# A graph layer, a mixer and an expert layer in one kernel: the targets' own rows as three bf16 parts, records zeroed ahead

## The chip, the cores and the metric

The kernel runs on one core of a Trainium2 chip. The metric is the device time of one execution in microseconds (us), the median of several executions. The engines are named as in the profile: PE is TensorE's matmuls and PEld its weight loads, DVE is VectorE, ACT is ScalarE, POOL is GpSimd, SP is SyncE, which here only issues DMAs.

## The reference

3125 nodes have 512 features each, and 50000 edges join them. The layer normalizes the rows, adds a message-passing layer and a linear-attention mixer, and then a layer of eight experts of which each row takes two. The change touches the message passing alone:

```python
edge_dst, edge_src = (edge_index[0], edge_index[1])
p0, p1 = split_irreps(irrep_linear(x, W_pre0, b_pre0, W_pre1))
pd0 = p0[edge_dst]
ip1 = einsum('eum,eum->eu', p1[edge_dst], p1[edge_src]) / 3.0
s0 = concatenate([pd0, pd0, ip1], -1)
w = ssp(edge_attr @ W_f1) @ W_f2 * (ssp(s0 @ W_s1) @ W_s2)
...                                                      # out0, out1 from w, x[edge_src] and edge_sh
out = segment_sum(edge_feat, edge_dst, num_segments=N)
```

For every edge one needs the row of its target (`pd0` through `W_s1` is 32 numbers, `p1` is 384) and the row of its other end. All is float32.

## The kernel before

The work has three parts in time.

**The sort (up to about 565 us).** The 3125 targets are cut into 25 tiles of 125, each tile into two halves of up to 64 targets. The kernel counts on the chip which half each edge belongs to and gives it a place, by matmuls of bf16 one-hots on PE and comparisons on DVE. Then each edge's record (48 floats: 4 spherical numbers, the index of the other end, the index of the target, its place in the half tile, and 32 hidden numbers from the edge's attributes) is written to its place in the DRAM table `recs` by indirect DMAs that POOL issues, 128 edges each (`place`, L529). All these puts wait for two DMAs that zero part of `recs` (`cleared`, L183): only the last quad of each tile and the quads for overflow. In the same stretch PE, DVE and ACT compute the node tables: `rows_d` (416 floats a node: the 32 and the 384 from above) and `rows_s` (896 floats), the mixer and the sums so far. The last DMAs of `place` follow without PE.

**The edges (about 565 to 1697 us).** Edges are worked on in *pairs* of two columns of 128 edges, one column from each half of a tile; two pairs make a *quad*, 104 in all. Eight pairs (four quads) belong to each of the 25 tiles, and eight pairs more, with a tile looked up at run time, hold what overflows (`late_tiles`). The order of the instructions on PE, ACT, DVE and POOL is that of the program (`manual_schedule`): one step `s` of a loop issues a stage of several different pairs, so that a pair passes through the stages over some 14 steps. SP's order is the scheduler's. The stages, with the names that matter:

- `load` brings the quad's records to `Q.rec`; `targets` brings a tile's 125 own rows from `rows_d` to `own` (SP, two DMAs of 64 rows, three buffers).
- `clear` (DVE, L1109) masks records of places that no edge took, with `real_slot`: what was not zeroed in DRAM is whatever lay there.
- `which` (DVE, L1142) makes the one-hot `one` of each edge's place among the 64 targets; `over` (PE L1150, ACT L1152) turns the first pair's into `oneT`.
- `fetch` gathers `gx` (rows of the other end, for both pairs) and `gd` (target rows, for the second pair alone) by indirect DMAs on POOL.
- `own_rows` (PE, L1163) spreads the tile's own rows over the first pair's edges by matmul with `oneT`, so that these need no gather; two row groups of 64 run side by side.
- `products` (DVE), `turn` (PE, L1182), `hidden` (PE, L1196 to L1211; L1206 is the targets' 32 numbers, for the first pair again from `own` with `oneT`), `softplus` (ACT).
- `scaled` (ACT, L1250) makes `ones`, the one-hot times each spherical number; `weigh` (PE L1262, L1263; ACT L1265; DVE L1266) the weights; `feats` (DVE L1280, L1284) the features; `gather_up` (PE, L1304) sums them by target into PSUM.

Matmuls whose operands are float32 are two PE instructions in the trace, those in transposing form and those in bf16 one.

**The experts (about 1697 us to the end)**, which the change leaves alone.

Of the kernel before, what the change touches and what calls it, by code (L numbers as in the profile page):

```python
# [17 lines left out]
P = 128  # L18
# [8 lines left out]
G = 4  # L27
# [24 lines left out]
def gnn_mix_moe_kernel(ctx: ExitStack, tc: tile.TileContext, a: dict, out: bass.AP):  # L52
# [41 lines left out]
    nc.vector.tensor_scalar(ident, jp, 0.0, None, op0=ALU.is_equal)  # L94
    after = const.tile([P, P], F32, name="after")
    nc.vector.tensor_scalar(after, jp, 0.0, None, op0=ALU.is_gt)
    ones = const.tile([P, P], F32, name="ones")
    nc.vector.memset(ones, 1.0)
    eps = const.tile([P, 1], F32, name="eps")
# [5 lines left out]
    real_slot = const.tile([P, NFIX + NOV_MOST, PR], I32, name="real_slot")  # L105


    rows_d = dram.tile([N + 2, HID + 3 * MUL], F32, name="rows_d")
# [34 lines left out]
    with ExitStack() as c1:  # L143
# [27 lines left out]
        for r in range(4):  # L171
# [5 lines left out]

        zero = tmp.tile([P, 3 * P], F32, name="zero")
        nc.vector.memset(zero, 0.0)
        by_quad = recs.rearrange("(q p i) f -> p q (i f)", p=P, i=G)  # L180
        per = PER // PR
        cleared = [
            nc.gpsimd.dma_start(by_quad[:, qs, :], zero[:, : G * REC].unsqueeze(1).to_broadcast([P, n, G * REC]))  # L183
            for qs, n in (
                (slice(per - 1, NFIX // PR, per), NG), (slice(NFIX // PR, (NFIX + NOV_MOST) // PR), NOV_MOST // PR),
            )
        ]
        for part in (slice(0, HID), slice(HID, HID + 3 * MUL)):
            nc.gpsimd.dma_start(rows_d[N:, part], zero[:2, : part.stop - part.start])
# [572 lines left out]
        w1t = c4.enter_context(tc.tile_pool(name="w1t", bufs=1, reuse_waits="tile"))  # L762


        def fixed_real():

            is_real = w1t.tile([P, NG, PER, 2], F32, name="is_real")
            nc.vector.tensor_tensor(
                is_real, slot_no[:, :PER].unsqueeze(1).unsqueeze(3).to_broadcast([P, NG, PER, 2]),
                held.unsqueeze(2).to_broadcast([P, NG, PER, 2]), op=ALU.is_lt,  # L770
            )
            nc.vector.tensor_single_scalar(
                real_slot[:, :NFIX, :].rearrange("p s k -> p (s k)"),
                is_real.rearrange("p b j k -> p (b j k)"), -1.0, op=ALU.mult,
            )
# [20 lines left out]
        def over_tiles(k):  # L796

            begun = w1t.tile([P, NOV], F32, name="begun", bufs=2)
            nc.vector.tensor_scalar(begun, pair_no, own_of[:, 2 + k : 3 + k], None, op0=ALU.is_ge)
            nc.vector.tensor_scalar(steps, ones, own_of[:, k : k + 1], None, op0=ALU.mult)  # L800
            ps = psum.tile([P, NOV], F32, name="ps_ov", tag="mm")
            nc.tensor.matmul(ps, steps[:NG, :], begun[:NG, :], start=True, stop=True)
            nc.vector.tensor_tensor(is_over, slot_no, ps, op=ALU.is_lt)
            late = w1t.tile([P, NOV], I32, name="late")
            nc.vector.tensor_single_scalar(late, is_over, -1.0, op=ALU.mult)
            nc.vector.tensor_copy(real_slot[:, NFIX:, k], late[:, :NOV_MOST])
# [88 lines left out]
        def lengths(c):  # L895
# [11 lines left out]
            8: [(composed,)], 9: [(fixed_real,), (over_steps,)], 10: [(over_tiles, 0)], 11: [(over_tiles, 1)],  # L907
        }
        for c in range(NCH):
            pieces.setdefault(2 * c, []).append((lengths, c))  # L910
# [167 lines left out]
    with ExitStack() as c2:  # L1078
# [53 lines left out]
        def targets(bs):  # L1132

            own = gat.tile([P, HID + 3 * MUL], F32, name="own", bufs=3)
            for k, b in enumerate(bs):
                nc.sync.dma_start(own[k * HT : (k + 1) * HT, :], rows_d[bass.ds(b * TG + k * (HT - 1), HT), :])
            return own

        def which(Q):

            Q.one = work.tile([P, G, HT], F32, name="one", bufs=5)
            nc.vector.tensor_tensor(  # L1142
                Q.one, lane[:, :HT].unsqueeze(1).to_broadcast([P, G, HT]),
                Q.rec[:, :, 6:7].to_broadcast([P, G, HT]), op=ALU.is_equal,
            )

        def over(Q):

            ps = ps_a.tile([P, G, P], F32, name="ps_one", tag="turned")
            nc.tensor.transpose(ps[:, 0, :], Q.one[:, :PR, :].rearrange("p k t -> p (k t)"), ident)  # L1150
            Q.oneT = work.tile([P, P], F32, name="oneT", bufs=4)
            nc.scalar.copy(Q.oneT, ps[:, 0, :])  # L1152

        def own_rows(R):

            if R.j == 1:
                R.gd = R.Q.gd[:, :, HID:]
                return
            ps = ps_a.tile([P, PR, D], F32, name="ps_gd")
            R.gd = ps[:, :, : 3 * MUL]  # L1160
            for k in range(PR):
                h = slice(k * HT, (k + 1) * HT)
                nc.tensor.matmul(  # L1163
                    R.gd[:, k, :], R.Q.oneT[h, :], R.own[h, HID:], start=True, stop=True,
                    tile_position=(k * HT, 0),
                )

        def products(R):

# [22 lines left out]
        def hidden(Q):  # L1192

            Q.ps = ps_a.tile([P, G, P], F32, name="ps_h", tag="turned")
            for i in range(G):
                nc.tensor.matmul(  # L1196
                    Q.ps[i * HID : (i + 1) * HID, 0, :], Q.rec[:, i, 8:USED], ident,
                    start=True, stop=True, tile_position=(0, i * HID),
                )
            for i in range(G):  # L1200
                h = slice(i % PR * HT, (i % PR + 1) * HT)
                if i < PR:
                    of, to, at = Q.gd[:, i, :HID], ident, 0
                else:
                    of, to, at = Q.pairs[0].own[h, :HID], Q.oneT[h, :], i % PR * HT
                nc.tensor.matmul(  # L1206
                    Q.ps[i * HID : (i + 1) * HID, 1, :], of, to, start=True, stop=False,
                    tile_position=(at, i * HID),
                )
            for i in range(G):  # L1210
                nc.tensor.matmul(  # L1211
                    Q.ps[i * HID : (i + 1) * HID, 1, :], w_s1c, Q.ip[:, i, :], start=False, stop=True,
                    tile_position=(0, i * HID),
                )
# [94 lines left out]
        def tile_of(engine, at):  # L1309

            return engine.value_load(at, min_val=0, max_val=NG - 1)
# [14 lines left out]
        with tc.manual_schedule(engines=steady):  # L1326
# [7 lines left out]
            def pair(at):  # L1334

                return [pairs[at]] if 0 <= at < n_pairs else []

            def late_tiles(at):

                return [pair_tile[0:1, k, at - NFIX : at - NFIX + 1] for k in range(2)]  # L1340
# [11 lines left out]
            for s in range(-LEAD - 5, n_pairs + 1):  # L1352
# [6 lines left out]
                for R in pair(s + LEAD + 3):  # L1359
                    at = s + LEAD + 3  # L1360
                    if at >= NFIX and R.j == 1:
                        continue
                    if at >= NFIX:
                        R.own = targets([tile_of(nc.sync, v) for v in late_tiles(at)])
                    elif at % PER == 0:
                        R.own = targets([at // PER] * 2)
                    else:
                        R.own = pairs[at - 1].own
                kept(s - 1)
                for Q in due(s + 2):  # L1370
                    softplus2(Q)
                for R in pair(s + 7):
                    products(R)
                for Q in due(s + LEAD + 1):
                    q = quads.index(Q)
                    clear(Q, real_slot[:, PR * q : PR * (q + 1), :])
                    which(Q)
                for Q in due(s + LEAD):
                    over(Q)
# [33 lines left out]
        with tc.If(some > NOV_MOST):  # L1413
            with tc.For_i(NOV_MOST // PR, (some + 1) // PR, 1) as i:
# [10 lines left out]
                for j in range(PR):  # L1425
                    R = Pair(Q, j)
                    fetch(Q, j)
                    if j == 0:
                        R.own = targets([tile_of(nc.sync, whose[:, k, j : j + 1]) for k in range(2)])
                    own_rows(R)  # L1430
                    products(R)
                turn(Q)
# [506 lines left out]
```

## Time and profile before

| | |
|---|---|
| median of 3 runs | 2573.27 us (2565.25 to 2579.46) |
| profiled execution | 2575.68 us, its span 2573.9 us |
| busy share of the span: PE, DVE, ACT, POOL | 91%, 64%, 49%, 59% |
| first put of a record, last put | 46.24 us, 564.21 us |
| PE's last matmul of the sort, its first of the edges | 479.89 us, 569.49 us |
| stretch 605 to 1650 us: PE, DVE, ACT, POOL busy | 1045, 970, 791, 668 us |
| `gather_up`, PE L1304 | 3328 matmul instructions, 493.8 us |
| `own_rows`, PE L1163, 900 to 1500 us | 228 matmul instructions of 535 ns, 52.2 us |

The span is that of the instructions; the execution's own time is 1.8 us more. Matmuls are pipelined, so their times overlap and the sum of a group's durations is more than the time from its first start to the next group's; starts are what to read.

### The profile page before, as it was taken

What the parts mean: (1) busy time and instruction counts of PE and PEld (TensorE: products, weight loads), DVE (VectorE), ACT (ScalarE), POOL (GpSimd) and SP (SyncE); (2) the same over time, 40 slices, a digit from 0 to 9 for tenths busy, and PEclk for the clock granted to TensorE, in tenths of its full rate; (3) what the DMA queues carried; (4) which work ended last, traced back from release to release, by engine and by line L of the source; (5) the groups of instructions that cost most, each with busy time, mean ns of one, the idle gap of its engine ahead of it and who ended that gap; (6) DMA issues with size and microseconds to landing.
All of it is one profiled execution on the core that took longest, in us unless ns stands there. A gap on an engine that the chain in (4) does not pass through costs nothing. (4 is left out here: it accounts for less than half of the span.)

```text
span 2573.9 us, 46654 instructions
## 1 busy us (share of the span) xinstructions
PE 2347.7 (91%) x16977; PEld 1522.1 (59%) x16977; DVE 1634.8 (64%) x3130; ACT 1254.0 (49%) x3444; POOL 1529.1 (59%) x1488
## 2 busy tenths in 40 slices
PE   6888999408999999999999999984999999999998
PEld 4654456304444444444444444463888888888887
DVE  8887444207999999999999999976222222222222
ACT  2665512105777777777777777752222222222221
POOL 3777767776666666666666666413555555555552
PEclk7999999758999999999999999997999999999999
DMA  4665889528777777777777777545315325857454
GB/s 145 189 209 198 303 294 312 191 65 262 231 229 232 229 230 228 231 229 231 230 228 227 233 228 231 175 164 209 107 51 183 131 56 192 332 186 258 140 171 143
DMA packets 188092, 521.94 MB, mean 203 GB/s; under 512 B 55421, under 2 KB 84166, under 8 KB 177104
## 3 DMA queue, kind: packets, MB, share of 16 engines
q0 software_dynamic: 110224, 397.55, 48.2%
q1 hardware_dynamic: 71296, 115.05, 13.6%
q10 hardware_dynamic: 6336, 6.28, 0.8%
q8 instruction: 137, 2.24, 0.3%
q14 instruction: 99, 0.81, 0.1%
HBM read 586.07 MB, written 104.25 MB: 268 GB/s over the span
## 5 line engine op out<-in xcount | busy, mean ns | idle before, releaser
L1127 POOL DMA_INDIRECT gx<-rows_s,rec x416 | 445.5, 1071 | 326.5 <-DVE ft L1284 217.7
L1304 PE MATMUL ps_s<-ft,ones 128*64 128x256 f32 (+1 forms) x3328 | 493.8, 439 | 10.0 <-DVE acc L1318 9.9
L1250 ACT ACTIVATE ones<-one,rec 128x64 f32<-128x64 f32 x1664 | 429.5, 337 | 0.0
L1800 PE MATMUL ps_f<-h,we 128*128 128x128 f32 x3328 | 394.4, 277 | 1.2 <-DVE h L1815 1.2
L1813 ACT ACTIVATE h<-ps_f,bias 128x128 f32<-128x128 f32 x312 | 114.5, 368 | 575.2 <-PE ps_f L1800 558.7
L529 POOL DMA_INDIRECT recs<-again,at_i x335 | 326.3, 974 | 113.9 <-issue 78.9
L1800 PEld LDWEIGHTS ps_f<-h,we 128*128 128x128 f32 x3328 | 379.8, 192 | 3.1 <-DVE h L1815 1.6
L1284 DVE TENSOR_TENSOR ft<-wt,gx 128x768 f32<-128x768 f32 x416 | 378.3, 951 | 0.0
L1815 DVE TENSOR_SCALAR h<-ps_f,bias 128x128 f32<-128x128 f32 x312 | 108.6, 350 | 422.7 <-PE ps_f L1800 419.0
L1304 PEld LDWEIGHTS ps_s<-ft,ones 128*64 128x64 f32 x3328 | 222.2, 136 | 228.3 <-issue 148.5
L1720 POOL DMA_INDIRECT we<-w_rows,w_at x208 | 211.6, 1017 | 215.4 <-PE ps_y L1832 93.3
L1266 DVE TENSOR_TENSOR wt<-wt,wb 128x1024 f32<-128x1024 f32 x208 | 253.2, 1217 | 59.7 <-ACT wt L1265 59.2
L1123 POOL DMA_INDIRECT gd<-rows_d,rec x208 | 252.6, 1214 | 64.6 <-issue 64.3
L1265 ACT COPY wt<-wa 128x1024 f32<-128x1024 f32 x208 | 211.3, 1016 | 126.2 <-PE wb L1263 126.2
L1262 PE MATMUL wa<-w_f,hT 32*128 32x512 f32 x832 | 236.8, 640 | 0.0
L1263 PE MATMUL wb<-w_s,hT 32*128 32x512 f32 x832 | 235.8, 640 | 0.0
L1800 PEld LDWEIGHTS ps_f<-xt,we 128*128 128x128 f32 x1664 | 195.4, 193 | 25.5 <-issue 23.7
L1800 PE MATMUL ps_f<-xt,we 128*128 128x128 f32 x1664 | 195.8, 276 | 0.7 <-ACT xt L1748 0.7
L1832 PE MATMUL ps_y<-we,h 128*128 128x512 f32 x416 | 192.4, 605 | 0.1
L1182 PEld LDWEIGHTS ps_ip<-ident,prod 128*128 128x128 f32 x1248 | 136.6, 142 | 78.7 <-ACT oneT L1152 77.2
L1182 PE MATMUL ps_ip<-ident,prod 128*128 128x128 f32 x1248 | 161.6, 280 | 0.7 <-ACT oneT L1152 0.7
L1280 DVE TENSOR_TENSOR ft<-wt,gx 128x512 f32<-128x512 f32 x208 | 144.0, 692 | 7.1
(394 smaller groups left out, 3282.2 us busy)
## 6 DMA issues: line engine op xcount, KB each, us to landing
w_rows<-in_Wh SPq DMA_DIRECT2D x24, 1024.0 KB
rows_s<-r SPq DMA_DIRECT2D x24, 448.0 KB
rec<-recs SPq DMA_DIRECT2D x104, 96.0 KB
w_rows<-in_Wo SPq DMA_DIRECT2D x8, 1024.0 KB
lined<-rec SPq DMA_DIRECT2D x12, 672.0 KB
again<-lined POOLq DMA_DIRECT2D x12, 672.0 KB
gx<-rows_s,rec POOLq DMA_INDIRECT x416
xs<-acc POOLq DMA_DIRECT2D x25, 256.0 KB
```

The source lines that it names most:

```text
L529: put = nc.gpsimd.indirect_dma_start(out=recs[:, :], out_offset=bass.IndirectOffsetOnAxis(ap=at_i[:m, t : t + 1], axis=0), in_=again[c][:m ...
L1123: nc.gpsimd.indirect_dma_start(out=Q.gd[:, i - 2, :], out_offset=None, in_=rows_d[:, :], in_offset=bass.IndirectOffsetOnAxis(ap=reci[:, i, ...
L1127: nc.gpsimd.indirect_dma_start(out=Q.gx[:, i, :], out_offset=None, in_=rows_s[:, :], in_offset=bass.IndirectOffsetOnAxis(ap=reci[:, i, 4:5 ...
L1182: nc.tensor.matmul(ps[:, i, :], Q.prod[:, i, b * P : (b + 1) * P], ident, is_transpose=True, start=(b == 0), stop=(b == 2),)
L1250: nc.scalar.activation(R.ones[:, k, c, :], R.Q.one[:, i, :], AF.Copy, scale=R.Q.rec[:, i, c : c + 1])
L1262: nc.tensor.matmul(wa[:, k, :], Q.hT[r, 0, :], w_f2[r, :], start=True, stop=True)
L1263: nc.tensor.matmul(wb[:, k, :], Q.hT[q, 1, :], w_s2[q, :], start=True, stop=True)
L1266: nc.vector.tensor_mul(R.wt, R.wt, wb)
L1284: nc.vector.tensor_mul(R.ft[:, k, MUL : 7 * MUL].rearrange("p (b c u) -> p b c u", b=2, c=3), w[:, k, :, 1, :].unsqueeze(2).to_broadcast([ ...
L1304: nc.tensor.matmul(to, R.ones[:, k, m, :], what, start=(first and m == 0), stop=(last and m == 3), tile_position=(0, k * HT),)
L1720: nc.gpsimd.indirect_dma_start(out=dst, out_offset=None, in_=src, in_offset=bass.IndirectOffsetOnAxis(ap=at[:, j : j + 1], axis=0), bounds ...
L1800: nc.tensor.matmul(pss[f], ws[l][:, k, f * P : (f + 1) * P], h[:, k, :], start=(k == 0), stop=(k == 3))
```

## The change

Four things are done.

1. The own rows of a tile are split into three bf16 parts that sum to them: ACT copies the rows to bf16 (`own_high`), DVE subtracts that from the rows (`own_rest`), ACT copies what is left to bf16 (`own_middle`), DVE subtracts again into the third part (`own_low`). This is done once for each tile, in four steps of the loop, ahead of use. The float32 rows have two buffers, the parts three.
2. The one-hot `one` and its turned form `oneT` are bf16. `over` is a bf16 matmul with a bf16 identity instead of a float32 transpose. `own_rows` and the targets' part of `hidden` accumulate three bf16 matmuls in place of each float32 one.
3. All 104 quads of `recs` are zeroed at the start, by four DMAs.
4. `clear`, `real_slot` and `fixed_real` go from the loop: the records are used as they come.

```diff
+    ident_b = const.tile([P, P], BF16, name="ident_b")
+    nc.vector.tensor_copy(ident_b, ident)
...
-        by_quad = recs.rearrange("(q p i) f -> p q (i f)", p=P, i=G)
-        per = PER // PR
+        n_zero = (NFIX + NOV_MOST) // PR * G * REC
+        step_z = zero.shape[1]
+        by_part = recs[: n_zero * P // REC, :].rearrange("(p i) f -> p (i f)", p=P)
         cleared = [
-            nc.gpsimd.dma_start(by_quad[:, qs, :], zero[:, : G * REC].unsqueeze(1).to_broadcast([P, n, G * REC]))
-            for qs, n in (
-                (slice(per - 1, NFIX // PR, per), NG), (slice(NFIX // PR, (NFIX + NOV_MOST) // PR), NOV_MOST // PR),
-            )
+            nc.gpsimd.dma_start(
+                by_part[:, i * n_zero // 4 : (i + 1) * n_zero // 4].rearrange("p (a b) -> p a b", b=step_z),
+                zero.unsqueeze(1).to_broadcast([P, n_zero // 4 // step_z, step_z]),
+            )
+            for i in range(4)
         ]
...
+        class Own:
+            def __init__(self, bs):
+                self.rows = gat.tile([P, OWN], F32, name="own", bufs=2)
+                for k, b in enumerate(bs):
+                    nc.sync.dma_start(
+                        self.rows[k * HT : (k + 1) * HT, :], rows_d[bass.ds(b * TG + k * (HT - 1), HT), :]
+                    )
+        def own_high(O):
+            O.parts = gat.tile([P, 3, OWN], BF16, name="own_b", bufs=3)
+            nc.scalar.copy(O.parts[:, 0, :], O.rows)
+        def own_rest(O):
+            nc.vector.tensor_sub(O.rows, O.rows, O.parts[:, 0, :])
+        def own_middle(O):
+            nc.scalar.copy(O.parts[:, 1, :], O.rows)
+        def own_low(O):
+            nc.vector.tensor_sub(O.parts[:, 2, :], O.rows, O.parts[:, 1, :])
...
-            Q.one = work.tile([P, G, HT], F32, name="one", bufs=5)
+            Q.one = work.tile([P, G, HT], BF16, name="one", bufs=5)
...
-            nc.tensor.transpose(ps[:, 0, :], Q.one[:, :PR, :].rearrange("p k t -> p (k t)"), ident)
-            Q.oneT = work.tile([P, P], F32, name="oneT", bufs=4)
+            nc.tensor.matmul(
+                ps[:, 0, :], Q.one[:, :PR, :].rearrange("p k t -> p (k t)"), ident_b, start=True, stop=True
+            )
+            Q.oneT = work.tile([P, P], BF16, name="oneT", bufs=4)
...
-            for k in range(PR):
-                h = slice(k * HT, (k + 1) * HT)
-                nc.tensor.matmul(
-                    R.gd[:, k, :], R.Q.oneT[h, :], R.own[h, HID:], start=True, stop=True,
-                    tile_position=(k * HT, 0),
-                )
+            for part in range(3):
+                for k in range(PR):
+                    h = slice(k * HT, (k + 1) * HT)
+                    nc.tensor.matmul(
+                        R.gd[:, k, :], R.Q.oneT[h, :], R.own.parts[h, part, HID:], start=(part == 0),
+                        stop=(part == 2), tile_position=(k * HT, 0),
+                    )
...
-                    of, to, at = Q.pairs[0].own[h, :HID], Q.oneT[h, :], i % PR * HT
+                    terms = [Q.pairs[0].own.parts[h, part, :HID] for part in range(3)]
+                    to, at = Q.oneT[h, :], i % PR * HT
...
+                for R in split(s + LEAD + 1):
+                    own_rest(R.own)
+                for R in split(s + LEAD):
+                    own_low(R.own)
...
-                    q = quads.index(Q)
-                    clear(Q, real_slot[:, PR * q : PR * (q + 1), :])
                     which(Q)
...
                 for R in pair(s + 2):
                     scaled(R, 1)
+                for R in split(s + LEAD + 2):
+                    own_high(R.own)
+                for R in split(s + LEAD + 1):
+                    own_middle(R.own)
```

More of the change, by code (lines that the diff above doesn't have):

```diff
@@ L104, in gnn_mix_moe_kernel @@
     pair_tile = const.tile([P, 2, NOV_MOST], I32, name="pair_tile")
-    real_slot = const.tile([P, NFIX + NOV_MOST, PR], I32, name="real_slot")
     rows_d = dram.tile([N + 2, HID + 3 * MUL], F32, name="rows_d")
@@ L179, in gnn_mix_moe_kernel @@
         nc.vector.memset(zero, 0.0)
-        by_quad = recs.rearrange("(q p i) f -> p q (i f)", p=P, i=G)
-        per = PER // PR
+        n_zero = (NFIX + NOV_MOST) // PR * G * REC
+        step_z = zero.shape[1]
+        assert n_zero % (4 * step_z) == 0
+        by_part = recs[: n_zero * P // REC, :].rearrange("(p i) f -> p (i f)", p=P)
         cleared = [
-            nc.gpsimd.dma_start(by_quad[:, qs, :], zero[:, : G * REC].unsqueeze(1).to_broadcast([P, n, G * REC]))
-            for qs, n in (
-                (slice(per - 1, NFIX // PR, per), NG), (slice(NFIX // PR, (NFIX + NOV_MOST) // PR), NOV_MOST // PR),
+            nc.gpsimd.dma_start(
+                by_part[:, i * n_zero // 4 : (i + 1) * n_zero // 4].rearrange("p (a b) -> p a b", b=step_z),
+                zero.unsqueeze(1).to_broadcast([P, n_zero // 4 // step_z, step_z]),
             )
+            for i in range(4)
         ]
@@ L762, in gnn_mix_moe_kernel @@
         w1t = c4.enter_context(tc.tile_pool(name="w1t", bufs=1, reuse_waits="tile"))
[L765 to L770, printed above, removed]
-            )
-            nc.vector.tensor_single_scalar(
-                real_slot[:, :NFIX, :].rearrange("p s k -> p (s k)"),
-                is_real.rearrange("p b j k -> p (b j k)"), -1.0, op=ALU.mult,
-            )
         is_over = w1t.tile([P, NOV], F32, name="is_over")
@@ L805, in over_tiles @@
             nc.vector.tensor_single_scalar(late, is_over, -1.0, op=ALU.mult)
-            nc.vector.tensor_copy(real_slot[:, NFIX:, k], late[:, :NOV_MOST])
             nc.sync.dma_start(late_real[k], late)
@@ L906, in gnn_mix_moe_kernel @@
             6: [(through, w_nn[0][:, 1, :], w_nn[0][:, 0, :], w_o[0])], 7: [(through, w_nn[1][:, 1, :], w_nn[1][:, 0, :], w_o[1])],
-            8: [(composed,)], 9: [(fixed_real,), (over_steps,)], 10: [(over_tiles, 0)], 11: [(over_tiles, 1)],
+            8: [(composed,)], 9: [(over_steps,)], 10: [(over_tiles, 0)], 11: [(over_tiles, 1)],
         }
@@ L1130, in fetch @@
                 )
[L1132 to L1137, printed above, removed]
+        OWN = HID + 3 * MUL
+        class Own:
[14 more added lines that the diff above has]
+            nc.vector.tensor_sub(O.parts[:, 2, :], O.rows, O.parts[:, 1, :])
         def which(Q):
-            Q.one = work.tile([P, G, HT], F32, name="one", bufs=5)
+            Q.one = work.tile([P, G, HT], BF16, name="one", bufs=5)
             nc.vector.tensor_tensor(
@@ L1160, in own_rows @@
             R.gd = ps[:, :, : 3 * MUL]
-            for k in range(PR):
-                h = slice(k * HT, (k + 1) * HT)
-                nc.tensor.matmul(
-                    R.gd[:, k, :], R.Q.oneT[h, :], R.own[h, HID:], start=True, stop=True,
-                    tile_position=(k * HT, 0),
-                )
+            for part in range(3):
[5 more added lines that the diff above has]
+                    )
         def products(R):
@@ L1202, in hidden @@
                 if i < PR:
-                    of, to, at = Q.gd[:, i, :HID], ident, 0
+                    terms, to, at = [Q.gd[:, i, :HID]], ident, 0
                 else:
-                    of, to, at = Q.pairs[0].own[h, :HID], Q.oneT[h, :], i % PR * HT
[L1206 to L1209, printed above, removed]
+                    terms = [Q.pairs[0].own.parts[h, part, :HID] for part in range(3)]
+                    to, at = Q.oneT[h, :], i % PR * HT
+                for j, of in enumerate(terms):
+                    nc.tensor.matmul(
+                        Q.ps[i * HID : (i + 1) * HID, 1, :], of, to, start=(j == 0), stop=False,
+                        tile_position=(at, i * HID),
+                    )
             for i in range(G):
@@ L1336, in pair, with split @@
                 return [pairs[at]] if 0 <= at < n_pairs else []
+            def split(at):
+                return [R for R in pair(at) if (at % PER == 0 if at < NFIX else R.j == 0)]
             def late_tiles(at):
@@ L1363, in gnn_mix_moe_kernel @@
                     if at >= NFIX:
-                        R.own = targets([tile_of(nc.sync, v) for v in late_tiles(at)])
+                        R.own = Own([tile_of(nc.sync, v) for v in late_tiles(at)])
                     elif at % PER == 0:
-                        R.own = targets([at // PER] * 2)
+                        R.own = Own([at // PER] * 2)
                     else:
@@ L1428, in gnn_mix_moe_kernel @@
                     if j == 0:
-                        R.own = targets([tile_of(nc.sync, whose[:, k, j : j + 1]) for k in range(2)])
+                        R.own = Own([tile_of(nc.sync, whose[:, k, j : j + 1]) for k in range(2)])
+                        own_high(R.own)
+                        own_rest(R.own)
+                        own_middle(R.own)
+                        own_low(R.own)
                     own_rows(R)
```

## The prediction

> **What bounds the kernel now.** I read the page's slices first, then the windows by stage, the timelines of PE and DVE in the middle of the edge stage, and POOL's timeline up to that stage. Slices of the page:
> ```profile
> PE   6888999408999999999999999984999999999998
> DVE  8887444207999999999999999976222222222222
> PEclk7999999758999999999999999997999999999999
> ```
> Window of the edge stage (columns: stretch, its length, then busy time and instructions of PE, PEld, DVE, ACT and POOL, the granted clock, DMA share, GB/s):
> ```profile
> 605.00:1650.00 1045.00, 1045.00 (x8794) 508.36 (x8794) 970.45 (x1287) 791.33 (x2399) 667.93 (x594) 1.00 0.75 230
> ```
> PE is busy all of 1045 us, at full clock; DVE 93%, ACT 76%, POOL 64%. A busy PE may still be one that waits between its matmuls, so the timeline of PE, and one line of its weight loads:
> ```profile
> 1006.53 0.41 PE L1206 MATMUL ps_h<-oneT,own 64*32 64x128 f32 x4
> 1006.87 0.43 PE L1211 MATMUL ps_h<-ip,w_s1c 128*32 128x128 f32 x8
> ...
> 1009.53 0.92 PE L1163 MATMUL ps_gd<-own,oneT 64*128 64x384 f32 x4
> 1010.38 0.33 PE L1150 MATMUL ps_one<-ident,one 128*128 128x128 f32 x1
> 1010.64 0.69 PE L1262 MATMUL wa<-w_f,hT 32*128 32x512 f32 x1
> ```
> ```profile
> 1009.53 0.30 PEld L1163 LDWEIGHTS ps_gd<-own,oneT 64*128 64x128 f32 x4 [0.38 <-issue]
> ```
> Each group starts where the one before it ends. The same group returns after 10.57 us (L1262 at 1000.07 and 1010.64), which is one quad of edges (four half tiles, two pairs): over 0.26, weigh 1.07, turn 1.46, gather_up 2.30, weigh 1.07, hidden 1.26, gather_up 2.30, own_rows 0.85. PE is the bound of this stage, and what is saved on PE shortens it until DVE binds. DVE over the same quad:
> ```profile
> 1002.31 1.22 DVE L1266 TENSOR_TENSOR wt<-wt,wb 128x1024 f32<-128x1024 f32 x1 [0.59 <-ACT wt L1265]
> ...
> 1006.98 0.32 DVE L1109 TENSOR_TENSOR rec<-rec,real_slot 128x160 int32<-128x160 int32 x1
> 1007.40 0.42 DVE L1142 TENSOR_TENSOR one<-lane,rec 128x256 f32<-128x256 f32 x1
> ...
> 1008.99 0.69 DVE L1280 TENSOR_TENSOR ft<-wt,gx 128x512 f32<-128x512 f32 x1
> 1009.60 1.82 DVE L1284 TENSOR_TENSOR ft<-wt,gx 128x768 f32<-128x768 f32 x2
> ```
> Its one wait in a quad is 0.59 us, so it has 9.98 us of work: only 0.59 us behind PE.
>
> The second stretch that matters is before it. POOL places the edges' records, one put each 1.26 us:
> ```profile
> 46.24 1.04 POOL L529 DMA_INDIRECT recs<-rec,at_i  x1 [37.97 <-DVE at_i L375]
> 337.09 0.96 POOL L529 DMA_INDIRECT recs<-again,at_i  x1 [6.83 <-PE ps_nn L1002]
> 569.68 1.05 POOL L1127 DMA_INDIRECT gx<-rows_s,rec  x1 [4.56 <-DVE one L1142]
> ```
> The last put is at 564, 84 us after PE's last matmul of that stage. Between 328 and 360 the puts wait 12.4 us for PE (2.30, 6.83, 2.19 and 1.08), so a later first put is absorbed up to 12 us, but a later PE chain is not.
>
> **PE, part by part.** The rates come from the sort, where both kinds stand side by side:
> ```profile
> 63.50 0.31 PE L339 MATMUL ps_at<-xT,after_b 128*128 128x350 bf16 x1
> 63.65 0.29 PE L340 MATMUL ps_at<-seen,ones_b 128*128 128x300 bf16 x1
> 63.78 0.31 PE L343 MATMUL ps_at<-starts,part_of 128*128 128x350 bf16 x1
> ...
> 64.35 1.88 PE L642 MATMUL ps_kx<-xn,kf 128*128 128x512 f32 x4
> 66.07 1.05 PE L419 MATMUL ps_h<-w_f,ea 128*128 128x128 f32 x8
> ```
> Bf16: 0.15 us for 350 columns and 0.13 for 300, 0.43 ns a column. F32: 1.72 us for four instructions of 512, 0.84 ns a column, and two instructions to a matmul. From bf16 to f32 and back costs nothing there.
> - own_rows: two f32 passes of 384 columns (its two row groups run side by side) are 0.645 us of the 0.85, so 0.20 is the group's own start and end. Three bf16 passes are 0.49, with the 0.20 again 0.69: 0.16 less.
> - hidden's own part: 0.34 us, of which 2 x 128 columns f32 0.215, so 0.125 fixed. Three bf16 passes 0.165, in all 0.29: 0.05 less.
> - over: 0.26, of which one pass of 128 f32 columns 0.107. In bf16 0.055: 0.05 less.
>
> In sum 0.26 us a quad. Bounds: if a bf16 load of 128 columns takes none of the fixed part, own_rows and over give another 0.05 each, 0.36; if the fixed part is paid for every pass, there is a loss (rival). I take 0.26, since the four f32 loads of L1163 above take 0.30 us in all and so lie beside matmuls that run 0.85: the later passes' loads are hidden, and each bf16 pass (0.16 us) is as long as half of that. 1045 / 10.57 = 99 quads: **-26 us**.
> [...]
>
> **DVE and ACT.** The clear of L1109 goes, 104 times: 0.42 us from its start to the next. Added for each target tile (25 fixed, 4 late; a tile lasts four quads) are two subtractions of 128x416 on DVE and two copies on ACT. No row mixes bf16 with f32 in a subtraction; by L1280 (0.61 us from start to start for 512) it is 0.50, and I bound it at 0.4 and, twice that row, 1.0. So DVE does 9.98 - 0.42 + 2 x 0.50 / 4 = 9.81 us a quad (10.06 at the dear end), under PE's new 10.31. The one-hot in bf16 has f32 operands still: same 0.42. ACT's copies, by L1190's 0.56 for 512, are 0.46: 0.23 a quad on an engine with 2.6 us idle. They stand behind `scaled` at the end of a step; queued behind them is ACT's copy of wa, then DVE's wt; feats ends at 1005.99 and its gather starts at 1007.23, and that 1.24 us covers half a microsecond. Without that cover it would be 0.5 us for 25 tiles, 12 us. The four late tiles' splits fall into the last steps of full PE: 1.0 us more on DVE in each of four quads (9.56 + 1.0 = 10.56 against 10.31), **+1**. The tail after 1650 is DVE's own and keeps its length. SP's loads of own rows have two buffers instead of three, but these are free after own_low, not after four quads: nothing waits longer.
> At the start, the gathers no longer wait for clear and one (568.56 to about 569.6, the 4.56 us row): **-1**.
>
> **The zeros.** Four DMAs on POOL's queue write all 104 quads, 128 x 13 x 384 x 4 bytes each, 10.2 MB instead of 2.85. POOL issues them in some 4 us of the 38 it sits idle. The DMA engines while they wrote the old zeros:
> ```profile
> 4.00:14.00 10.00, 4.35 (x13) 1.88 (x13) 9.37 (x26) 0.00 (x0) 2.88 (x5) 1.00 1.03 330
> ```
> Full, at 330 GB/s, of which the zeros some 270. From 14 to 22 us the share was 0.59, from 22 to 46 0.30. At 270 GB/s the new zeros end at 4 + 38 = 42 us, before the first put (which waits for them). But all that is loaded meanwhile for the sort goes at a fraction: `ea` for PE at 21.80, x for DVE at 36.73, W_kT for PE at 40.07, all ahead of the first put on their in-order engines. The bounds are 0 and, if nothing of ea lands before 42, +20. I take **+4**, near the lower end, since ea, sh and W_kT also moved while the DMA was full.
> [...]
>
> Sum: -26 + 1 - 1 + 4 = -22. The profiled execution took 2575.7 (span 2573.9), 2.4 above the median, so 2553.7 there and **2551** as a median.
>
> **Rivals.**
> 1. Slower: every accumulating pass shows its load. Where: own_rows and hidden, two further passes each. If a pass adds half the group's fixed share, own_rows is 0.49 + 0.20 + 2 x 0.10 = 0.89 and hidden's part 0.41: with over -0.05, +0.06 a quad, +6 us, with the zeros about 2583. If all of it, 1.09 and 0.54: +0.39 a quad, +39, about 2616. It eats the saving from 0.065 us a pass. Against it: the loads of L1163. Chance 0.10.
> 2. DVE binds: its 0.59 us wait for ACT stays, as it hangs on weigh and the copy of wa, which keep their length. Then a quad is 9.56 + 0.25 + 0.59 = 10.40: 17 us saved instead of 26, 2560. Against: PE reaches weigh earlier after a shorter own_rows and over. Chance 0.13.
> 3. The zeros starve the sort: +20 instead of +4, 2567. For: x and ea are needed before 42 us. Chance 0.10.
> That the change does not do what it says is excluded by the order of the built instructions: no clear is left, each own_rows is six loads and six matmuls.
>
> **How the numbers follow.** The forecast has 0.67, its own range 2536 (PE at 0.36 a quad, zeros free) to 2562. Measurable from no change is about 0.5%, 13 us: faster is below 2560, slower above 2586. Faster: 0.63 of the forecast and 0.07 of rival 2, 0.70. Slower: 0.09, the most of rival 1 and a little for zeros far slower than any row. Same: the rest, 0.21. The range is 2534 to 2574: up to rival 3, leaving out rival 1.
>
> **What would show it.** Right: own_rows from start to next group 0.69, over 0.21, hidden's part 0.29, a quad of 10.31 with PE still full and DVE at 95%; first put at about 50 us, last at about 568. Wrong: weight loads of L1163 that start only when the matmul before has ended; idle PE ahead of gather_up; a first put well behind 50.

## The result, and the profile after

The changed kernel takes 2538.72 us (median of 4 runs, 2536.73 to 2541.63) against 2570.20 for the kernel before, run beside it (4 runs): 31.5 us less, a ratio of 0.9875, 95% interval 0.9855 to 0.9894. The forecast was 2551, its range 2534 to 2574. The profiled execution took 2537.24 us, its span is 2535.5: 38.4 less than before's 2573.9, where the sum of the prediction had 22 less. The profiled pair differs by more than the medians, since before's profiled execution lay 5.5 us above its median and after's 1.5 below.

The slices of the changed kernel's page look like those of before:

```profile
PE   5888989507999999999999999966999999999998
...
PEclk7999999857999999999999999987999999999999
```

The window of the edge stage (stretch, length, busy time and instructions of PE, PEld, DVE, ACT, POOL, granted clock, DMA share, GB/s):

```profile
605.00:1600.00 995.00, 995.00 (x9089) 493.00 (x9090) 955.58 (x1227) 805.02 (x2428) 654.94 (x588) 1.00 0.77 239
```

PE is still full and DVE at 96%: PE still sets the pace. From the first gather of the edges to the end of the last sum kept, before took 1132.6 us (569.68 to 1702.29) and after 1092.1 (569.93 to 1662.05). So 40.5 us came off this stage; the stages behind it gave back 1.8, the sort 0.3. Over 85 quads a quad went from 10.573 to 10.160 us, 0.413 less where 0.26 was forecast, and 98 times that is the 40.5.

PE's timeline in the middle of the stage, and the weight loads of `own_rows` (L1173):

```profile
999.97 0.43 PE L1206 MATMUL ps_h<-ident,rec 128*32 128x128 f32 x8
...
1000.53 0.35 PE L1218 MATMUL ps_h<-oneT,own_b 64*32 64x128 bf16 x6
1000.81 0.43 PE L1223 MATMUL ps_h<-ip,w_s1c 128*32 128x128 f32 x8
1001.17 2.37 PE L1316 MATMUL ps_s<-ft,ones 128*64 128x512 f32 x16
...
1003.47 0.66 PE L1173 MATMUL ps_gd<-own_b,oneT 64*128 64x384 bf16 x6
1004.07 0.23 PE L1157 MATMUL ps_one<-ident_b,one 128*128 128x128 bf16 x1
1004.23 0.69 PE L1274 MATMUL wa<-w_f,hT 32*128 32x512 f32 x1
```
```profile
1003.47 0.28 PEld L1173 LDWEIGHTS <-oneT 64*128 64x128 bf16 x6 [0.39 <-issue]
```

From start to the next start: `own_rows` 0.60 (before 0.85, forecast 0.69), `over` 0.16 (0.26, forecast 0.21), the own rows' part of `hidden` 0.28 (0.34, forecast 0.29). These three are 0.25 + 0.10 + 0.06 = 0.41: the whole of the gain. All six loads of `own_rows` are through 0.28 us after the group's start, while its matmuls go on for 0.60.

DVE over part of that quad, and its waits in the window above (us in total, times, longest):

```profile
1005.62 0.59 DVE L1144 TENSOR_TENSOR own_b<-own,own_b 128x416 bf16<-128x416 f32 x1
1006.12 0.95 DVE L1185 TENSOR_TENSOR prod<-ps_gd,gx 128x768 f32<-128x768 f32 x1
```
```profile
DVE wt L1278 <- ACT wt L1277: 27.1, 47, 0.6
```

The subtraction costs 0.50 from start to start, as estimated. DVE's wait for ACT's copy of wa has not gone; in before it came 97 times in 605 to 1650, 57.3 us. It was forecast to be filled, or else to hold PE up. It stays in half the quads, and PE does not wait for it.

The start, by windows, POOL's timeline and two lines of other engines that waited for loads:

```profile
4.00:14.00 10.00, 3.32 (x11) 1.41 (x11) 9.32 (x26) 0.00 (x0) 5.55 (x7) 1.00 1.04 380
14.00:22.00 8.00, 4.78 (x24) 2.49 (x22) 8.00 (x6) 0.00 (x0) 0.00 (x0) 1.00 1.03 408
22.00:46.00 24.00, 14.13 (x64) 9.86 (x63) 18.88 (x56) 5.34 (x11) 0.00 (x0) 0.65 0.73 283
```
```profile
51.44 1.05 POOL L533 DMA_INDIRECT recs<-rec,at_i  x1 [40.31 <-DVE at_i L379]
...
569.93 1.06 POOL L1118 DMA_INDIRECT gx<-rows_s,rec  x1 [4.22 <-DMA rec<-recs]
```
```profile
24.09 2.04 PE L423 MATMUL ps_h<-w_f,ea 128*128 128x128 f32 x8 [1.99 <-issue]
...
42.48 0.69 DVE L559 BATCH_NORM_STATS2 bn<-x 128x6 f32<-128x512 f32 x1 [3.64 <-DMA x<-in_x]
```

The DMA engines are full (a share of 1.02 to 1.04), at 380 to 418 GB/s, until 34 us; from there to 36 us the share is 0.81. By the semaphore records the last zeros landed at 45.1 us (42 in the prediction), and the first put waited another 6 us for `at_i`, which DVE computes: what made it late is not the zeros' own landing, but, as far as these lines show, the late loads ahead of it. PE gets `ea` 2.3 us later than before (24.09 against 21.80) and DVE gets x 5.8 us later, 3.64 of it shown as a wait. The first put moves from 46.24 to 51.44, but the last put's end only from 565.13 to 565.71: the puts that follow made up 4.6 us. Some 3.5 of these come off their waits for PE between 328 and 360 us, which were 12.4 us in before and are 8.9 now (6.04, 1.20 and 1.69); the rest is spread over small waits.

### The profile page after: what moved, and what is told of

Its sections match the earlier page's. It is cut to its first block, busy times and chain, and to the rows that moved or that the text cites. A ratio compares the mean times of both kernels' runs of the same rounds, so it can differ in the third digit from the quotient of the medians.

```text
span 2535.5 us, 47384 instructions
## 1 busy us (share of the span) xinstructions
PE 2309.5 (91%) x17393; PEld 1515.2 (60%) x17393; DVE 1631.8 (64%) x3081; ACT 1277.7 (50%) x3502; POOL 1524.6 (60%) x1490
## 5 line engine op out<-in xcount | busy, mean ns | idle before, releaser
L1316 PE MATMUL ps_s<-ft,ones 128*64 128x256 f32 (+1 forms) x3328 | 494.2, 439 | 10.2 <-DVE acc L1330 10.2
L1262 ACT ACTIVATE ones<-one,rec 128x64 f32<-128x64 bf16 x1664 | 429.2, 337 | 0.0
```

The source lines that it names most:

```text
L1262: nc.scalar.activation(R.ones[:, k, c, :], R.Q.one[:, i, :], AF.Copy, scale=R.Q.rec[:, i, c : c + 1])
L1316: nc.tensor.matmul(to, R.ones[:, k, m, :], what, start=(first and m == 0), stop=(last and m == 3), tile_position=(0, k * HT),)
```

## The experiments

They ran on three chips, each with its own runs of the kernel before, with which alone its times are compared. A quad's time is that of one profiled execution. On the first chip before took 2572 to 2589 us, on the second 2767 to 2833, on the third 2780 to 2829. That difference became a question of its own.

### First chip: which part of the change is worth what

**The clear put back, with a mask that clears nothing** (after, with DVE's clear in each quad again):

```diff
+    all_set = const.tile([P, PR, PR], I32, name="all_set")
+    nc.vector.memset(all_set, -1)
...
                 for Q in due(s + LEAD + 1):
+                    clear(Q, all_set)
                     which(Q)
```

> The changed kernel with one clear a quad on DVE put back (a mask of all ones, so nothing else changes). PE theory: the 0.41 us that a quad lost (10.57 to 10.16) came from the bf16 groups on PE. DVE's own work a quad is 9.81 + 0.42 = 10.23 us with the clear, so DVE now binds: a quad of 10.23 to 10.40, 25 to 34 us under the kernel before less what the start costs, ratio 0.987 to 0.993. DVE theory (the 0.41 saved is the 0.42 of the clear, PE only looked full): a quad back at 10.57, ratio 1.00.

**The zeros and the missing masks alone, in float32** (before, with after's zeroing and without `clear`):

```diff
-            nc.gpsimd.dma_start(by_quad[:, qs, :], zero[:, : G * REC]...
+            nc.gpsimd.dma_start(by_part[:, i * n_zero // 4 : (i + 1) * n_zero // 4]...
...
-                    clear(Q, real_slot[:, PR * q : PR * (q + 1), :])
                     which(Q)
```

> The kernel before with only the other half of the change: all records zeroed ahead, no masks, own rows and one-hots still float32. PE theory: a quad stays at 10.57, since PE's groups are as before; first put 5 us later and absorbed; ratio 0.999 to 1.001. DVE theory: a quad of 10.15, 40 us less, ratio 0.985.

**One change of tile shape less in `hidden`** (after, with the products by `w_s1c` straight behind gd's, which have the same shape, and the own rows' six bf16 passes last):

```diff
-            for i in range(G):
+            for i in range(PR):
...
             for i in range(G):
                 nc.tensor.matmul(
-                    Q.ps[i * HID : (i + 1) * HID, 1, :], w_s1c, Q.ip[:, i, :], start=False, stop=True,
+                    Q.ps[i * HID : (i + 1) * HID, 1, :], w_s1c, Q.ip[:, i, :], start=(i >= PR), stop=(i < PR),
                     tile_position=(0, i * HID),
                 )
+            for i in range(PR, G):
+                h = slice(i % PR * HT, (i % PR + 1) * HT)
+                for part in range(3):
+                    nc.tensor.matmul(
+                        Q.ps[i * HID : (i + 1) * HID, 1, :], Q.pairs[0].own.parts[h, part, :HID], Q.oneT[h, :],
+                        start=False, stop=(part == 2), tile_position=(i % PR * HT, i * HID),
+                    )
```

> The changed kernel with the order inside hidden turned: the four products with w_s1c (128 rows by 32 columns) straight behind those of the same shape, the targets' bf16 passes (64 by 32) last. One change of tile shape in a quad fewer. If each such change costs the 0.09 to 0.10 us that stand between a group's last stream and the next load, hidden falls from 1.20 to about 1.06 and a quad to 10.03 to 10.07, where DVE with 9.81 does not yet bind: 9 to 13 us under the changed kernel. If DVE binds already (27 us of waits for ACT's copy are left), 0 to 4 us.

**The changed kernel again**, on the same chip:

> The changed kernel as it is, on the same chip as the other three, to compare them with. A quad of 10.16, ratio 0.986 to 0.989 to the kernel before.

| first chip, before 2581.32 us (17 runs) | us | ratio, 95% interval | quad, us |
|---|---|---|---|
| clear put back | 2549.29 | 0.988 (0.9857 to 0.9904) | 10.160 |
| zeros without masks, float32 | 2585.81 | 1.0022 (1.0005 to 1.0039) | 10.573 |
| `w_s1c` products first | 2530.37 | 0.980 (0.9773 to 0.9826) | 10.023 |
| after again | 2542.58 | 0.9855 (0.9831 to 0.9878) | 10.160 |

The window of the edge stage, first of the kernel with the clear put back, then of the zeros in float32:

```profile
605.00:1600.00 995.00, 995.00 (x9080) 495.28 (x9076) 977.28 (x1322) 803.59 (x2425) 674.59 (x588) 1.00 0.78 239
```
```profile
605.00:1600.00 995.00, 995.00 (x8375) 483.47 (x8379) 893.48 (x1132) 752.30 (x2281) 653.15 (x566) 1.00 0.77 231
```

Of the latter kernel also DVE's wait in that window:

```profile
DVE wt L1255 <- ACT wt L1254: 95.0, 93, 1.0
```

With the clear back, DVE is busy 977 of 995 us, its waits for ACT's copy of wa are gone, and the quad is still 10.160, below all that was expected of it: DVE's work with the clear is thus at most 10.16 us a quad, not 10.23. The median is 6.7 us above after's, with intervals that overlap; in the profiles that difference lies in the sort (first gather at 570.10 against 560.83). So DVE's clear was never on the path: without it DVE waits, with it DVE works. Taking it away in float32 shows the same from the other side: DVE falls to 893 us, its waits for ACT rise to 95.0 us in 93 times, and the quad stays at 10.573. What that kernel has besides are the zeros, and it is 0.2% slower (1.3 to 10 us; at most 0.1% was expected). The gain is thus in the bf16 passes alone.

The reordered kernel, in PE's timeline:

```profile
1009.23 0.43 PE L1206 MATMUL ps_h<-ident,rec 128*32 128x128 f32 x8
...
1010.01 0.35 PE L1223 MATMUL ps_h<-oneT,own_b 64*32 64x128 bf16 x6
1010.29 2.38 PE L1316 MATMUL ps_s<-ft,ones 128*64 128x512 f32 x16
```

`hidden` is 1.06 us instead of 1.20 (999.97 to 1001.17 above), and the edges are 12 us shorter than in the changed kernel's profile on this chip (1081.7 against 1093.6), as are the medians. The matmuls are the same; what went is one switch between a tile of 128 rows and one of 64, with whatever load stood behind it. The expected 1.06 came true, and the quad fell a little more than expected. On this chip that version beats both kernels. The changed kernel again came out at 0.9855, just under the 0.986 to 0.989 expected, with the quad as expected.

### Second chip: what a pass and its load cost

**The first bf16 part alone** (two of three passes, and the later casts and subtractions, left out):

```diff
-            for part in range(3):
+            for part in range(1):
...
-                    terms = [Q.pairs[0].own.parts[h, part, :HID] for part in range(3)]
+                    terms = [Q.pairs[0].own.parts[h, part, :HID] for part in range(1)]
```

> The changed kernel with the first bf16 part alone: the second and third part are left out, their two subtractions, their copy and the two further passes of own_rows and of hidden with them. If a pass costs its stream and nothing else (384 columns at 0.43 ns, 128 at 0.43 ns, loads hidden), own_rows falls from 0.60 to 0.27, hidden's own part from 0.28 to 0.17, a quad from 10.16 to 9.72. If loads show in each pass (the first rival, at half price), own_rows falls to about 0.17 and a quad to 9.5. DVE without the subtractions has 9.48 of work a quad and does not bind at 9.72.

**`own_rows` with weights of 96 columns instead of 128:**

```diff
-                        R.gd[:, k, :], R.Q.oneT[h, :], R.own.parts[h, part, HID:], ...
+                        R.gd[:96, k, :], R.Q.oneT[h, :96], R.own.parts[h, part, HID:], ...
```

> The changed kernel with 96 instead of 128 columns of oneT as own_rows' weights (the products of the other 32 rows are zeros from GpSimd instead, so that part is left out). The streams are the same 384 columns three times. If a bf16 load is nearly free whatever its width (theory 1), the first pass still takes 0.17 us from its load to the second pass and the group 0.60. If only full loads of 128 columns are that quick (theory 2), the first load takes 96 columns at 0.4 to 0.85 ns, 0.04 to 0.08 us instead of 0.01: the group 0.63 to 0.67.

**After with the old zeroing** (2.85 MB instead of 10.2):

```diff
-            nc.gpsimd.dma_start(by_part[:, i * n_zero // 4 : (i + 1) * n_zero // 4]...
+            nc.gpsimd.dma_start(by_quad[:, qs, :], zero[:, : G * REC]...
```

> The changed kernel with the old, smaller zeroing (2.85 MB instead of 10.2), still without masks; on these inputs every place left empty lies in what is zeroed. If the later first put is absorbed by the waits for PE behind it, the first put is back at 46 us and the time stays within 3 us of the changed kernel. If the zeros hold the sort up, by the 3.6 us for x and the 2 us for ea, 4 to 6 us less than the changed kernel.

**The changed kernel again:**

> The changed kernel beside few_zeros on the same chip. Edges of about 1093 us from the first gather to the last kept sum, ratio 0.985 to 0.989.

| second chip, before 2792.32 us (23 runs) | us | ratio, 95% interval | quad, us |
|---|---|---|---|
| one part | 2712.67 (one run) | | 10.61 |
| 96 columns | 2815.35 (one run) | | 11.44 |
| old zeroing | 2782.70 | 0.9977 (0.9949 to 1.0004) | 11.33 |
| after again | 2784.50 | 0.9995 (0.9966 to 1.0023) | 11.30 |

By the starts of their matmuls the groups are as on the first chip. One part takes 0.27 us in `own_rows` and 0.16 in `hidden`, against 0.60 and 0.28 with three: 0.163 and 0.059 us a further pass, about its stream alone (384 and 128 columns at the sort's 0.43 ns a column are 0.165 and 0.055). The median starts within `own_rows` are 0, 0.173 and 0.336 us for the three passes; with 96 columns 0, 0.200 and 0.363. So 0.010 us of a load shows in the first pass, 0.037 with fewer columns, and none in the other two in either kernel. The whole group takes 0.62 us with 96 columns: not the 0.60 of theory 1, and just under the 0.63 to 0.67 of theory 2. A load of 96 columns takes longer, 0.119 us against 0.094.

But nearly nothing of the gain is left on this chip: the ratio is 0.9995, where 0.985 to 0.989 was expected, and a quad 11.30. One part alone took 0.69 off a quad where the starts give 0.44, and so missed the 9.72 expected of it. With the old zeroing the first put is back at 46.57 us, as expected, but what the zeros cost is too little to be told here (2782.70 against 2784.50).

### Third chip: where the gain went on the slower chips

**Before, for its profile:**

> The kernel before, unchanged, for its profile beside the runs of this call. The question is a stretch that the one-part and the three-part kernels showed where before took some 2790 us: ScalarE's copy of the hidden values (hT) there began a median 2.3 us after the last hidden product was issued, not 0.34 us, though every matmul was issued at the usual spacing, and a quad took 11.30 us where its matmuls' spacing adds up to 10.16. Theory A, TensorE's array runs behind what is issued to it there, and the more so the more bf16 passes there are: if before takes over 2700 us in this call, its quad is 11.3 to 11.5 (1.08 of 10.57), so that the change has next to nothing to win; if before takes about 2575, its quad is 10.57 and the copy begins 0.34 us after the last product. Theory B, the three parts' own chain through ScalarE and VectorE is what is late there: before, which has no such chain, has 10.57 and 0.34 us in either case.

**After:**

> The changed kernel, unchanged, once more against the kernel before. Theory A: a ratio of 0.985 to 0.990 and a quad of 10.16 us if hT's copy begins 0.34 us after the last hidden product was issued, a ratio of 0.995 to 1.003 and a quad of about 11.3 if it begins over 1 us after it. Theory B expects the second ratio over 1.01 in the second case, since before would have no such wait.

**One part:**

> The first bf16 part alone (own rows' products are then rounded to bf16; the two other parts, their casts and subtractions are left out): 8 of 12 bf16 passes of a quad less, which are 0.33 us in own_rows (0.60 to 0.27) and 0.12 us in hidden (0.28 to 0.16) by the spacing of their starts. Theory A: if hT's copy begins 0.34 us after the last hidden product, the passes cost their spacing, and the quad is 9.72 us, 0.44 less than with three parts, some 2495 us in all; VectorE, with 0.25 a quad less to do, has 9.64 and does not bind. If the copy begins late, the passes cost more than their spacing, as in the look before (11.30 to 10.61, 0.69 us for 0.44). A rival, VectorE binds at 9.9 to 10: the quad is 9.9 or more, some 2515 us, with TensorE waiting.

**The `w_s1c` products first:**

> The changed kernel with hidden's products by w_s1c moved ahead of the own rows' bf16 passes, so that one change of tile shape is left out: again. If the copy begins at its usual distance from the last product, a quad of 10.02 us, 0.14 less than the changed kernel, and a ratio of 0.979 to 0.983. If TensorE's array runs behind, a change of shape costs no more and no less there: a quad 0.1 to 0.2 us under the changed kernel's, and a ratio of 0.985 to 0.995.

| third chip, before 2806.71 us (19 runs) | us | ratio, 95% interval | quad, us | hT's copy after the last hidden product's issue, median us |
|---|---|---|---|---|
| before, profiled | 2780.99 (one run) | | 11.30 | 2.56 |
| after | 2806.67 | 0.9974 (0.9928 to 1.0019) | 11.37 | 2.39 |
| one part | 2707.41 | 0.9642 (0.9569 to 0.9715) | 10.57 | 1.21 |
| `w_s1c` products first | 2796.26 | 0.9968 (0.9935 to 1.0001) | 11.30 | 2.23 |

In the reordered kernel that copy began 0.27 us after the last product on the first chip, in the others that ran there 0.34.

Before, on this chip, in a window of the edge stage, in PE's timeline and then in ACT's:

```profile
800.00:1800.00 1000.00, 962.92 (x7889) 468.83 (x7885) 873.62 (x1154) 697.26 (x2143) 598.56 (x532) 1.00 0.70 215
```
```profile
999.20 0.59 PE L1263 MATMUL wb<-w_s,hT 32*128 32x512 f32 x1
...
1000.62 0.42 PE L1211 MATMUL ps_h<-ip,w_s1c 128*32 128x128 f32 x8
...
1011.64 0.43 PE L1211 MATMUL ps_h<-ip,w_s1c 128*32 128x128 f32 x8
```
```profile
1001.68 1.01 ACT L1265 COPY wt<-wa 128x1024 f32<-128x1024 f32 x1 [2.56 <-PE ps_h L1211]
...
1003.40 0.37 ACT L1219 COPY hT<-ps_h 128x256 f32<-128x256 f32 x1 [0.71 <-remote]
...
1012.14 0.37 ACT L1219 COPY hT<-ps_h 128x256 f32<-128x256 f32 x1
```

ACT's copy of wa waits for the weigh group, whose last matmul was issued at 999.20: it starts 2.5 us later, after 2.56 us of idleness. In before's profile at the top (the one that the prediction reads) the same step takes 0.64 (1000.62 to 1001.26). The copy of hT waits for the last eight product instructions of `hidden` (L1211). At 1012.14 it starts 0.34 us after the last of them was issued, as all 86 such copies of before do in its profile at the top (700 to 1600 us). At 1003.40 it comes 2.6 us after, with 0.71 of idleness and the rest behind the late copy of wa. The sums of ACT's waits in 800 to 1800 us (total, times, longest):

```profile
ACT hT L1219 <- remote: 80.8, 49, 3.3
ACT wt L1265 <- PE ps_h L1211: 47.1, 22, 2.6
```

Theory B fails: before, which has no chain of three parts, waits like this too and has a quad of 11.30. Theory A has its numbers for before, after and one part: PE's results come later than its issue says, in all of these kernels. That they come the later the more bf16 passes there are is not borne out: before has no such pass in `own_rows` and `hidden`, and its 2.56 us is above after's 2.39. The median spacing of the issued matmuls within a group is unchanged (0.85, 0.26 and 0.34 in before). The quad's additional 0.7 us are waits that come now and then: in before 0.26 us a quad on average ahead of `turn`, mostly for ACT's `oneT` as far as the records tell, 0.17 within `hidden` and 0.15 within `gather_up`. PE is no longer busy throughout: 963 of 1000 us in the window above. For the last hidden product of one quad, the trace's semaphore records show the lateness without ACT: signalled 0.32 us after its issue in after's profile at the top (960.325 to 960.641), 2.26 us after it on the second chip (1055.322 to 1057.583, after again). A rival would be that the signals of every engine come late there. The same records speak against it. In before's profile on the third chip, 1555 of PE's 2727 signalling matmuls have a signal within 60 ns of their modelled end (2542 signals are on record), against 2722 in its profile at the top; of the signals on record of ACT and DVE, all but 8 of 3419 come within 60 ns of an instruction's end, as at the top. (A quarter of these two engines' signals is missing from that trace, so that "remote" in the waits above says no more than that the releaser is not on record.) The lateness is not confined to the edges either: the first gather came at 646.24 us there, against 569.68.

The reordered kernel misses its expectation: its quad is 0.07 under after's, not 0.1 to 0.2, and its ratio 0.9968 lies above 0.985 to 0.995. Its median is 10 us under after's, 12 on the first chip, but here the two intervals overlap, and executions of one kernel spread by 23 to 49 us, 0.2 to 0.5 us a quad: what the reorder is worth on this chip is open. The whole change gains at most 0.7% here and 0.3% on the second chip by the intervals, against 1.2 to 1.7% on the first. Only the kernel with one part gains clearly, and more than its spacing (0.80 for 0.44 in the profiled quads). Why is not shown. That matmuls cost more there than their spacing would not explain it alone: the change also takes streams away, 0.26 us a quad by the prediction's sums, and gains nothing clear; and the kernel with one part also spares DVE two subtractions and ACT a copy for each tile, which no run separates from the matmuls. The granted clock of the edges, their start and end with them, is 0.98 in before's profile here and 0.99 in that at the top, and 1.00 in the window above, which doesn't account for 11.30 against 10.57. What other cores of those chips did is unknown. What makes PE's results late, and why on some chips, stays open.

## Why the prediction was right, and where it was off

**Sign and cause: right.** PE was the bound, the bf16 passes shortened it, and nothing else became the bound: in after PE is busy 995 of 995 us. The time, 2538.72 us, lies 2.7 us inside the lower end of the prediction's own range, 2536, and that is partly luck. A quad fell by 0.41 us, more than the 0.36 on which this end rests, which is 5 us in all; the stages behind gave back 1.8 us that no term had, and the rest lies within the spread of single executions.

**PE's -26 us: too small by 15.** The mis-sized term is the fixed share of a group. The prediction took 0.20 us of `own_rows` for "the group's own start and end" and carried it over unchanged; its bound of 0.36 a quad let it shrink by 0.05. It shrank by 0.10. In before, the starts within `own_rows` are 0.427 us from first to second pass, of which 0.32 is stream. What is left, some 0.11, is taken for the load of 128 float32 columns that the first pass waits for: the next load starts 0.109 us after it. The end takes 0.097. In after the first pass is 0.173 (0.163 of stream, 0.010 of load) and the end 0.091. So half of the fixed share was a float32 load, and in bf16 it is nearly gone; the 96-column run, where 0.037 of it shows again, bears this out. In `over` the second 0.05 is put down to the same, but no run separates it there. The prediction had looked at the four loads' total, 0.30 us, and concluded that the later ones are hidden. That was right; the first was not, and it is the one that bf16 shortened.

**Rival 1, every accumulating pass shows its load: fell.** Passes 2 and 3 start 0.163 us apart, their stream. A load lies beside a matmul of its own row group here: two row groups have three loads each, and all six are through at 0.28 us. The last two run from 0.18 to 0.28 us, while the second pass of their own row groups streams (0.173 to 0.336).

**Rival 2, DVE's wait stays and binds: half true.** The wait stayed, but the price was wrong: 10.40 was put on it, and the quad is 10.16. The wait is slack that DVE has because PE sets the pace, not work. The run with the clear put back shows it: DVE's busy time rose by 22 us, its wait of 27 us went, and the quad did not move.

**The zeros, +4.** The first put was forecast at about 50 us and came at 51.44, but the last put only 0.6 us later, not 4. The prediction itself had named the cover, 12 us of waits for PE between 328 and 360, and the sum did not use it. These waits did shrink, by some 3.5 us. One profile says 0.6; the timed pair in float32 says 1.3 to 10 us. In the profiles on the first chip, of kernels with the same sort, the last put ended anywhere from 557 to 569 us, so a single profile can't settle this term. Rival 3 (+20) is out.

**The rest.** The forecast 1 us earlier start of the edges was 0.3 us later with the last put, and the late tiles' +1 can't be told apart in the 40.5.

## What to carry to other kernels

Split a matmul group's time into stream, visible load and end before changing its type: the load that the first matmul of a group waits for can change with the type too. In `own_rows` what shows of it went from some 0.11 us to 0.010, beside the 0.16 that the streams saved (0.645 to 0.49). An engine's wait just below the bound can be slack, as DVE's 27 us were here; put work into it to find out whether it matters (22 us more of DVE's work left the quad at 10.160), rather than adding the wait to the engine's work. And a gain measured on one chip may be absent on another: the ratio was 0.9855 on the first chip, 0.9995 and 0.9974 on the two where results came late after issue, and there only the kernel with fewer matmuls gained more than the spread of the runs (0.9642 on the third).

## What the runs showed of the hardware that was not expected

- A weight load of 64 rows by 128 columns took 0.184 us in float32 and 0.094 in bf16, but with 96 bf16 columns 0.119: a longer load for fewer columns. No run shows why.
- One change of tile shape fewer in `hidden`, with the load behind it, was worth 0.14 us a quad (10.160 to 10.023), 12 us in all, with the same matmuls, on the first chip. On the third chip it can't be told from the spread of the runs.
- On two of the three chips of the experiments the same program took 8 to 9% longer; there, on the third chip, ACT's copy of hT began a median 1.21 to 2.56 us after the last hidden product's issue, against 0.27 to 0.34 on the first, at a granted clock of 0.97 to 1.00 in the windows read. PE's signals came late there (1555 of 2727 signalling matmuls within 60 ns of their modelled end, in before on the third chip), and those of ACT and DVE that are on record did not (all but 8 of 3419). What made the difference is not known.
